# Four layers on one core: a matmul product in another bank, operators built later, a branch flag read earlier, and a fifth buffer

## The chip, the cores and the metric

The kernel runs on one core of one Trainium2 chip. The time is the device time in microseconds of one execution; a kernel's time is the median of several runs. A profile of one execution gives the spans and waits that are quoted. TensorE (PE) multiplies matrices, VectorE (DVE) and ScalarE (ACT) work on vectors, GpSimd (POOL) does slower vector work and issues some transfers, SyncE (SP) issues most transfers.

## The reference

The input is eight images of 512 channels by 32 by 32 pixels, in float32. Four layers follow each other:

- Layer 0: group norm over 8 groups; q, k, v by 512 x 512 weights; attention with 8 heads over the 1024 pixels; then three times `hf = hf + 0.1 * tanh(hf @ inl_w.T + inl_b)`; a 512 x 512 projection; and the layer's input is added.
- Layer 1: attention with one head, with 64 channels for q and k and 512 for v; and its input is added.
- Layer 2: a bias; upsampling by two with a 12-tap filter in both directions; leaky ReLU times the square root of two; downsampling by two with a 12-tap filter.
- Layer 3: the mean of each channel gives, through a router and a sigmoid, the weights of eight experts; the mixed kernels are used in a 1x1, a 3x3 and a 1x1 convolution, each with its scale and bias, ReLU after the first two; the layer's input is added, and a last ReLU follows.

## The kernel before, in words

`tile_sequence` computes all of it. A first loop goes over the images: `layer0`, `layer1`, and `layer2` for all but the last image; the results of layer 2 are spilled to DRAM. Then comes `layer2` of the last image, and a loop over the images for layer 3. The code gives a program order; the planner of the tile framework decides how the instructions of different stages are mixed on each engine, and each engine then takes its own in that order. A tile is taken from a ring of buffers; it can be written when the readers of the ring's buffer are done.

The rings that matter here. PSUM has three: `ps_mm` and `ps_tp` with two banks each, `ps_sc` with two pairs of banks. In SBUF, `big` has seven buffers, `tmp` of 1024 columns has four, `half` (a `tmp` of 512 columns) two.

The large products are done with seven half-size products in place of eight (`product`): from the four quarters of the weights and of the data it forms sums (`weight_sums` on GpSimd, `quarter_sums` on DVE), and adds up the seven products P1, C11, U2, U3, C22, C21, C12 in three pairs of banks, A (from `ps_mm`), X and Y (from `ps_sc`). P1 and C11 need no sums of the data. The trace names these banks: `inl_A`, `inl_X` and `inl_Y` are those of the inner loop, whatever the iteration.

In layer 0's attention a group is two heads and half of the query pixels. `weighted` adds its product in one bank of `ps_mm`; `normalised` takes one bank of `ps_tp` for the totals (L638), the reciprocal (L642), and multiplies into `hf` (L643), which reads and so frees the `ps_mm` bank. The inner loop's first product follows the last group. Its A banks are both from `ps_mm`.

Layer 2 is done by matmuls with small operators: `up_left_op`, `up_op`, `up63_op` for upsampling, `dn_op`, `dn63_op` for downsampling. `layer2_constants` builds them from the filters' taps, with some 360 small DVE instructions on a scratch tile `setup`, and clears the border rows of the padded image in DRAM (`ypad`, by `rim0`). It is called in layer 1 of the first image, ahead of the scores. `weighted_rows` is layer 1's product of weights and values (its matmuls are the `av` of L853, its sums are `av_U`, `av_W`, `av_P`); layer 2's matmuls are `up` (L919) and `dn` (L940), and `leak` (L902 on ACT, L903 on DVE) reads the upsampling banks.

No maximum is subtracted ahead of the exponentials. In place of it, GpSimd adds all their sums into `seen`; at the end, the kernel counts whether all are within a bound, loads the answer into a register of each engine (L1175), and a branch (L49) repeats everything with shifts where they are not. With the inputs used it isn't taken.

Of the kernel before, what the change touches and what calls it, by code (L numbers as in the profile page):

```python
# [9 lines left out]
F32 = mybir.dt.float32  # L10
BF16 = mybir.dt.bfloat16
AF = mybir.ActivationFunctionType
ALU = mybir.AluOpType
AX = mybir.AxisListType
# [3 lines left out]
P = 128  # L18
B, C, H, W = 8, 512, 32, 32
S = H * W  # L20
CC = C // P
SC = S // P
HALF = 512
# [18 lines left out]
BOUND = 1e20  # L42
# [11 lines left out]
def tile_sequence(ctx: ExitStack, tc: tile.TileContext, a: dict, out: bass.AP, shifted: bool):  # L54
    nc = tc.nc
# [4 lines left out]
    work = ctx.enter_context(tc.tile_pool(name=f"work_{run}", bufs=2))  # L60
    small = ctx.enter_context(tc.tile_pool(name=f"small_{run}", bufs=4))
    spill = ctx.enter_context(tc.tile_pool(name=f"spill_{run}", bufs=1, space=DRAM))
    ps_sc = ctx.enter_context(tc.tile_pool(name=f"ps_sc_{run}", bufs=2, space=PSUM))
    ps_tp = ctx.enter_context(tc.tile_pool(name=f"ps_tp_{run}", bufs=2, space=PSUM))
    ps_mm = ctx.enter_context(tc.tile_pool(name=f"ps_mm_{run}", bufs=2, space=PSUM))

    def big_tile(name, shape):
        return big.tile(shape, F32, tag="big", name=name)

    def bank(pool=None, name="mm"):  # L70
        pool = pool or ps_mm
        return pool.tile([P, HALF], F32, tag="bank", name=name)

    def tmp(name, n=HALF):
        if n == HALF:
            return work.tile([P, n], F32, tag="half", name=name, bufs=2)
        return work.tile([P, n], F32, tag="tmp", name=name, bufs=4)

    def sums(name):
        return work.tile([P, S], F32, tag="sums", name=name, bufs=2)  # L80
# [50 lines left out]

    def layer2_constants():

        setup = big_tile("setup", [P, CC * S])
        used = [0]

        def scratch(name, n):
            used[0] += n
            return setup[:, used[0] - n : used[0]]

        def iota(name, pattern, base, per_partition=0):
            t = scratch(name, pattern[0][1])
            nc.gpsimd.iota(
                t, pattern, base=base, channel_multiplier=per_partition,
                allow_small_or_imprecise_dtypes=True,
            )
            return t

        def placed(name, idx, taps):
            n = idx.shape[1]  # L150
            t, one = scratch(f"placed_{name}", n), scratch(f"one_{name}", n)
            for k in range(NTAP):
                dst = t if k == 0 else one
                nc.vector.tensor_scalar(
                    dst, idx, float(k), taps[:, k : k + 1], ALU.is_equal, ALU.mult
                )
                if k:
                    nc.vector.tensor_add(t, t, one)
            return t

        taps_up = scratch("taps_up", NTAP)
        nc.gpsimd.dma_start(taps_up, a["up_filter"].partition_broadcast(P))
        nc.vector.tensor_scalar_mul(taps_up, taps_up, 2.0)
        taps_dn = scratch("taps_dn", NTAP)
        nc.gpsimd.dma_start(taps_dn, a["down_filter"].partition_broadcast(P))

        part = iota("part", [[1, 1]], 0, 1)

        def rows_of(name, width):

            row, step = scratch(f"row_{name}", 1), scratch(f"step_{name}", 1)
            nc.vector.memset(row, 0.0)
            for k in range(width, P, width):
                nc.vector.tensor_scalar(step, part, float(k), None, ALU.is_ge)
                nc.vector.tensor_add(row, row, step)
            col = scratch(f"col_{name}", 1)
            nc.vector.scalar_tensor_tensor(col, row, float(-width), part, ALU.mult, ALU.add)
            return row, col

        def tap_index(name, n, step, base, mul, by):  # L180

            t = iota(f"ix_{name}", [[step, n]], base)
            add = scratch(f"add_{name}", 1)
            nc.vector.tensor_scalar_mul(add, by, float(mul))
            nc.vector.tensor_scalar_add(t, t, add)
            return t

        def outer(op, rows, cols):
            nr, ncol = rows.shape[1], cols.shape[1]
            nc.vector.tensor_tensor(  # L190
                op.rearrange("p (r c) -> p r c", c=ncol),
                rows.unsqueeze(2).to_broadcast([P, nr, ncol]),
                cols.unsqueeze(1).to_broadcast([P, nr, ncol]),
                ALU.mult,
            )

        in_c, in_r = rows_of("in", IR)
        ur = placed("ur", tap_index("ur", UR, -1, 17, -2, in_r), taps_up)
        outer(up_op, ur, placed("uc", tap_index("uc", UC, 1, 11, -2, in_c), taps_up))
        outer(
            up_left_op, ur, placed("ucl", tap_index("ucl", UC, 1, 11 - 2 * EDGE, -2, in_c), taps_up)
        )
        up_rr, up_cc = rows_of("up", UC)  # L210
        outer(
            dn_op,
            placed("dr", tap_index("dr", OR, 2, -6, 1, up_rr), taps_dn),
            placed("dc", tap_index("dc", OC, 2, 0, -1, up_cc), taps_dn),
        )
        in_c, in_r = rows_of("in63", 3)
        outer(
            up63_op,
            placed("ur63", tap_index("ur63", 1, 0, 10, -2, in_r), taps_up),
            placed("uc63", tap_index("uc63", 2 * W, 1, 5, -2, in_c), taps_up),  # L220
        )
        outer(
            dn63_op,
            placed("dr63", iota("dr63", [[2, 3]], 1), taps_dn),
            placed("dc63", tap_index("dc63", W, 2, 6, -1, part), taps_dn),
        )

        rim0 = tmp("rim0")
        nc.vector.memset(rim0, 0.0)
        for t in ypad:  # L230
            nc.gpsimd.dma_start(t[0 : 3 * W], rim0[0 : 3 * W])
            nc.gpsimd.dma_start(t[(H + 3) * W :], rim0[0 : 2 * W])


    ypad = [
        spill.tile([(H + 5) * W, C], F32, name=f"ypad_{run}_{i}", tag=f"ypad_{i}") for i in range(2)
    ]


    pooled = const.tile([P, CC, B], F32, name="pooled")  # L240
# [138 lines left out]
            nc.vector.tensor_sub(t[3][cc], t[1][cc], b21)  # L379
        return t  # L380

    def product(name, wt, src, sums_of, made, rows=False):

        banks = {
            "A": [bank(name=f"{name}_A{u}") for u in range(2)],
        }
        for key in "XY":
            two = ps_sc.tile([P, S], F32, tag="scores", name=f"{name}_{key}")  # L390
            banks[key] = [two[:, ts(u, HALF)] for u in range(2)]
# [30 lines left out]
    def all_of(gen):  # L422
        for _ in gen:
            pass
# [141 lines left out]
    def layer0(b, x, norm, w):  # L566
# [11 lines left out]
        w["proj"] = weight("proj", b)  # L578
        all_of(product(f"v_{b}", w["v"], h, t, positions(f"v_{b}", v, v_row), rows=True))
        w["v1"] = weight("v1", b)  # L580

        hf = big_tile(f"hf_{b}", [P, CC, S])
        rows = [slice(HD * r, HD * r + HD) for r in range(2)]
        shifts = None
# [73 lines left out]
        for it in range(3):  # L658
            t = quarter_sums(f"hf_{b}_{it}", hf, None if it else v)
            name = f"inl_{b}_{it}"  # L660
            all_of(product(name, w["inl"], hf, t, inner_step(name, hf)))
        if b + 1 < B:
            w["q"] = weight("q", b + 1)
        t = quarter_sums(f"hf_{b}_3", hf)
# [4 lines left out]
    def layer1(b, x, w, midway):  # L669
# [29 lines left out]
            )  # L699
        v = big_tile(f"v1_{b}", [P, SC, C])  # L700
        eT = [big_tile(f"eT_{b}_{sh}", [P, SC, HALF]) for sh in range(2)]
        if b == 0:
            layer2_constants()
        inv = small.tile([P, SC], F32, tag="inv1", bufs=2, name=f"inv1_{b}")
        accs = {}

# [74 lines left out]
                midway()  # L781

        weighted_rows(b, eT, v, inv, y, written)
        for t in range(3, NT):
            halo.load(t)
        halo.load_last()
# [299 lines left out]
    def mixed(b):  # L1086
# [10 lines left out]
                )  # L1097
        return wt

    z3 = {}  # L1100

    def freed(t):
# [8 lines left out]

    z_last = layer2(B - 1, halo, freed)
    z_next = z3[0]
    wt_next = mixed(0)
    route(B - 1, B)
    for b in range(B):
# [28 lines left out]
        for oc in range(CC):  # L1145
            at = C + 9 * P + oc * P
            ps = ps_sc.tile([P, S], F32, tag="scores", name=f"c3_{b}_{oc}")
            for g in range(2):
                nc.tensor.matmul(
                    ps[:, ts(g, HALF)], wt[:, at : at + P], h2[:, ts(g, HALF)],  # L1150
                    start=True, stop=True,
                )
            n = S if b + 1 < B else HALF
            for part in range(S // n):
                dst = z[:, oc, ts(part, n)]
                nc.vector.scalar_tensor_tensor(
                    dst, ps[:, ts(part, n)], bn[2][0][:, oc : oc + 1], dst, ALU.mult, ALU.add
                )
                nc.scalar.activation(dst, dst, AF.Relu, bias=bn[2][1][:, oc : oc + 1])
            nc.sync.dma_start(out[b, ts(oc, P), :], z[:, oc, :])  # L1160

    if shifted:
        return None

    within = tmp("within")
    nc.vector.tensor_scalar(within, seen, BOUND, None, ALU.is_le)
    count = small.tile([P, 1], F32, tag="count", name="count")
    nc.vector.tensor_reduce(count, within, AX.X, ALU.add)  # L1170
    ps = bank(name="within")
    nc.tensor.matmul(ps[0:1, 0:1], count, ones[:, 0:1], start=True, stop=True)
    redo = small.tile([P, 1], mybir.dt.int32, tag="redo", name="redo")
    nc.vector.tensor_scalar(redo[0:1, :], ps[0:1, 0:1], P * HALF - 0.5, None, ALU.is_lt)
    return nc.values_load(redo[0:1, 0:1], min_val=0, max_val=1)  # L1175


def _layout(inp):
# [64 lines left out]
```

## Time and profile before

| what | us |
|---|---|
| time, median of three runs | 3965.67 |
| lowest and highest | 3965.24, 3966.4 |
| span of the profiled execution | 3956.6 |
| DVE busy | 2592.0 |
| ACT busy | 1104.7 |
| GpSimd busy | 437.9 |

The span goes from the first to the last instruction of the profiled execution. A line of the timeline gives the start, the duration, the engine, the line of the kernel, the operation, what it writes from what it reads, the shape and how many were joined; in brackets, how long the engine had been idle and what ended that. The view of waits sums such idle times by pairs. The chain of work goes back from the last instruction to what released each step. A float32 matmul appears as two passes, each counted.

### The profile page before, as it was taken

The numbers are of one execution on the slowest core, as the hardware profiler recorded it, in microseconds if no ns is written. First come the engines' busy times: TensorE is split into PE (matmuls) and PEld (weight loads), VectorE is DVE, ScalarE is ACT, GpSimd is POOL, SyncE is SP. The second block draws the span as 40 slices with busy tenths as digits, with TensorE's granted clock in tenths as the row PEclk, the third lists the DMA queues.
The fourth block names the chain that finished last, engine by engine and source line by source line (L and its number), as shares of the span: only waits on it lengthen the run. The fifth ranks groups of instructions, "written<-read, shape, count | busy, mean of one in ns | idle before, by whom it ended". The sixth has DMA issues, their size and how long they took to land.

```text
span 3956.6 us, 37918 instructions
## 1 busy us (share of the span) xinstructions
PE 3873.8 (98%) x14630; PEld 2036.0 (51%) x14630; DVE 2592.0 (66%) x3690; ACT 1104.7 (28%) x1507; POOL 437.9 (11%) x310
## 2 busy tenths in 40 slices
PE   8998999999999999999999999999999999999998
PEld 4335753476435763367434764357534764346543
DVE  4779548764676647765486646765477655766885
ACT  1421214212332114212241223322142123321332
POOL 5310003000120003100030002200030001201000
PEclk9999999999999999999999999999999999999999
DMA  5002310113101310023101220013200131003432
GB/s 189 19 7 78 105 71 1 40 62 114 38 1 59 117 59 19 0 83 114 56 1 58 75 85 36 0 69 107 78 1 24 61 115 54 1 0 115 159 140 95
DMA packets 85214, 247.85 MB, mean 63 GB/s; under 512 B 10416, under 2 KB 32960, under 8 KB 78240
## 3 DMA queue, kind: packets, MB, share of 16 engines
q1 hardware_dynamic: 69136, 220.23, 15.6%
q10 hardware_dynamic: 13824, 12.59, 0.9%
q0 software_dynamic: 2064, 12.51, 0.8%
q8 instruction: 117, 1.92, 0.2%
q14 instruction: 73, 0.60, 0.0%
HBM read 185.40 MB, written 59.90 MB: 62 GB/s over the span
## 4 chain that ended last, share of the span: by engine, by line
PE 91%; DVE 6%; ACT 1%; DMA 1%; issue 1%; POOL 0%; ACTq 0%; SPq 0%; DVEq 0%; POOLq 0%
PE scores L264 13%; PE av L628 11%; PE inl_X L414 6%; PE dn L940 6%; PE up L919 5%; PE v_X L414 4%; PE inl_Y L414 4%; PE av_X L853 4%; PE inl_A L414 3%; PE c L1135 3%; PE v_Y L414 3%; PE av_Y L853 3%; PE av_A L853 2%; PE proj_X L414 2%; PE q_X L414 2%; PE k_X L414 2%
## 5 line engine op out<-in xcount | busy, mean ns | idle before, releaser
L613 ACT ACTIVATE e<-scores 128x1024 f32<-128x1024 f32 x512 | 497.4, 1022 | 583.0 <-PE scores L264 580.3
L619 DVE TENSOR_TENSOR acc<-acc,e 128x1024 f32<-128x1024 f32 x384 | 494.0, 1287 | 123.5 <-ACT e L613 103.4
L264 PE MATMUL scores<-q,k 64*128 64x512 f32 x2048 | 511.1, 616 | 6.0 <-DVE v L495 3.3
L628 PE MATMUL av<-e,v 128*64 128x512 f32 x2048 | 494.2, 605 | 0.0
L645 POOL TENSOR_TENSOR seen<-seen,acc 128x512 f32<-128x512 f32 x128 | 213.6, 1669 | 1565.0 <-DVE acc L619 1560.0
L264 PEld LDWEIGHTS scores<-q,k 64*128 64x128 f32 x2048 | 176.0, 186 | 333.1 <-ACT e L613 162.1
L628 PEld LDWEIGHTS av<-e,v 128*64 128x64 f32 x2048 | 124.9, 136 | 338.7 <-issue 336.4
L903 DVE SCALAR_TENSOR_TENSOR up<-up,leak 128x512 f32<-128x512 f32 (+1 forms) x264 | 174.5, 686 | 141.8 <-ACT leak L902 136.5
L940 PEld LDWEIGHTS dn<-dn_op,up 128*128 128x128 f32 (+1 forms) x2048 | 240.2, 192 | 44.0 <-issue 24.2
L940 PE MATMUL dn<-dn_op,up 128*128 128x126 f32 (+5 forms) x2048 | 244.7, 275 | 7.6 <-DVE up L903 6.8
L642 DVE RECIPROCAL inv<-total 128x512 f32<-128x512 f32 x64 | 214.7, 3355 | 0.0
L902 ACT ACTIVATE leak<-up 128x512 f32<-128x512 f32 (+1 forms) x264 | 150.1, 595 | 208.2 <-DVE up L903 131.0
L414 PE MATMUL inl_A<-hf,w_inl 128*128 128x512 f32 x384 | 178.0, 599 | 10.7 <-DVE hf L643 10.7
L919 PE MATMUL up<-halo,up_op 126*128 126x512 f32 (+1 forms) x384 | 182.6, 604 | 0.9 <-DVE up L903 0.8
L414 PE MATMUL inl_X<-T_hf,w_inl 128*128 128x512 f32 x384 | 175.2, 592 | 0.0
L645 POOL TENSOR_TENSOR seen<-seen,inv 128x512 f32<-128x512 f32 x64 | 125.2, 1956 | 416.9 <-DVE inv L642 416.9
L617 DVE TENSOR_TENSOR acc<-e,e 128x1024 f32<-128x1024 f32 x64 | 83.0, 1297 | 102.5 <-ACT e L613 102.5
L508 ACT ACTIVATE inl_U<-inl_U,inl_b 128x512 f32<-128x512 f32 x96 | 66.7, 718 | 287.4 <-DVE inl_U L523 287.4
L519 DVE TENSOR_TENSOR inl_U<-inl_X,inl_P 128x512 f32<-128x512 f32 x96 | 61.8, 685 | 111.4 <-PE inl_X L414 111.4
L737 POOL TENSOR_TENSOR seen<-seen,acc 128x512 f32<-128x512 f32 x16 | 23.4, 1461 | 987.7 <-DVE acc L729 921.5
L414 PEld LDWEIGHTS inl_A<-hf,w_inl 128*128 128x128 f32 x384 | 70.4, 190 | 110.2 <-issue 95.3
L1135 PE MATMUL c<-rim,mixed 128*128 128x512 f32 x288 | 124.9, 592 | 0.0
(302 smaller groups left out, 5779.0 us busy)
## 6 DMA issues: line engine op xcount, KB each, us to landing
halo<-ypad_u SPq DMA_DIRECT2D x128, 252.0 KB
halo<-ypad_u SPq DMA_DIRECT2D x128, 198.0 KB
w_v<-stored_u_v SPq DMA_DIRECT2D x14, 1792.0 KB
x<-in_x_dram SPq DMA_DIRECT2D x32, 512.0 KB
out_dram<-z SPq DMA_DIRECT2D x32, 512.0 KB
spill_u<-z SPq DMA_DIRECT2D x28, 512.0 KB
z<-spill_u SPq DMA_DIRECT2D x28, 512.0 KB
w_q<-stored_u_q SPq DMA_DIRECT2D x7, 1792.0 KB
```

Source lines behind the costliest of these rows:

```text
L264: nc.tensor.matmul(ps[r], k[r], q[r], start=True, stop=(shift is None))
L414: nc.tensor.matmul(dst, lhs, rhs, start=(opens and s == 0 and cc == 0), stop=(cc == 1 and s == rows), skip_group_check=True,)
L613: nc.scalar.activation(e, ps, AF.Exp, scale=HD ** -0.5)
L619: nc.vector.tensor_add(accs[g], accs[g], e)
L628: nc.tensor.matmul(avs[g][rows[r]], v[:, jc, ts(2 * oc + r, HD)], e[:, ts(r, HALF)], start=(jc == 0), stop=(jc == SC - 1),)
L642: nc.vector.reciprocal(inv, ps)
L645: nc.gpsimd.tensor_add(seen, seen, part)
L853: nc.tensor.matmul(ps[:, ts(s, QR)], left[:, j, at : at + P], right[:, j, :], start=(what in ("P1", "U2", "W") and s == 0 and j == 0), sto ...
L903: nc.vector.scalar_tensor_tensor(dst, ps, SQRT2, t, ALU.mult, ALU.max)
L919: nc.tensor.matmul(ps[i], op[0 : IR * n, :], halo.tile(t)[0 : IR * n, c + i, :], start=True, stop=True,)
L940: nc.tensor.matmul(rows[:, r0 - first : r1 + 1 - first, c0 : c1 + 1], up[t][0:k, c, ts(cc, P)], op[:, r0 - 4 * t + 3 : r1 + 4 - 4 * t, c0 ...
L1135: nc.tensor.matmul(banks[g].rearrange("p (h w) -> p h w", w=W), wt[:, at : at + P], h1[:, ky + 16 * g : ky + 16 * g + 16, kx : kx + W], st ...
```

## The change

Four edits, and some that go with them:

- The inner loop's first product takes its A banks one from `ps_mm` and one from `ps_tp`, the ring of the totals, so that neither is the one that the last group's `av` still holds.
- `layer2_constants` is called after `weighted_rows`, shortly ahead of the layer that needs the operators. Its scratch tile is a `tmp` of 1024 columns in place of a `big` one. Clearing the border rows is taken out of it and put at the beginning of the kernel.
- The flag for the branch is worked out after layer 2 of the last image, ahead of layer 3's loop, in a function `out_of_bounds`; the last image's output is written in halves of a channel block, as each is ready. In the built program, SyncE's load of the flag stands ahead of the load of the second image for layer 3; on the other engines the load is still the last instruction ahead of the branch.
- `tmp` has five buffers.

```
-        return work.tile([P, n], F32, tag="tmp", name=name, bufs=4)
+        return work.tile([P, n], F32, tag="tmp", name=name, bufs=5)
...
     def layer2_constants():
-        setup = big_tile("setup", [P, CC * S])
+        setup = tmp("setup", S)
...
-        rim0 = tmp("rim0")
-        nc.vector.memset(rim0, 0.0)
-        for t in ypad:
-            nc.gpsimd.dma_start(t[0 : 3 * W], rim0[0 : 3 * W])
-            nc.gpsimd.dma_start(t[(H + 3) * W :], rim0[0 : 2 * W])
...
+    rim0 = tmp("rim0")
+    nc.vector.memset(rim0, 0.0)
+    for t in ypad:
+        nc.gpsimd.dma_start(t[0 : 3 * W], rim0[0 : 3 * W])
+        nc.gpsimd.dma_start(t[(H + 3) * W :], rim0[0 : 2 * W])
...
-        banks = {
-            "A": [bank(name=f"{name}_A{u}") for u in range(2)],
-        }
+        banks = {"A": first_banks or [bank(name=f"{name}_A{u}") for u in range(2)]}
...
-            all_of(product(name, w["inl"], hf, t, inner_step(name, hf)))
+            banks = None if it else [bank(p, f"{name}_A{u}") for u, p in enumerate((ps_mm, ps_tp))]
+            all_of(product(name, w["inl"], hf, t, inner_step(name, hf), first_banks=banks))
...
-        if b == 0:
-            layer2_constants()
...
         weighted_rows(b, eT, v, inv, y, written)
+        if b == 0:
+            layer2_constants()
...
     z_last = layer2(B - 1, halo, freed)
     z_next = z3[0]
+    redo = None if shifted else out_of_bounds()
     wt_next = mixed(0)
...
-            nc.sync.dma_start(out[b, ts(oc, P), :], z[:, oc, :])
-    if shifted:
-        return None
-    within = tmp("within")
...
-    return nc.values_load(redo[0:1, 0:1], min_val=0, max_val=1)
+                nc.sync.dma_start(out[b, ts(oc, P), ts(part, n)], dst)
+    return redo
```

The part of the old end that is cut above (comparison, count, one matmul, and the load into registers) is the body of `out_of_bounds`, with its bank from `ps_tp`.

More of the change, by code (lines that the diff above doesn't have):

```diff
@@ L138, in scratch @@
             used[0] += n
+            assert used[0] <= S, used
             return setup[:, used[0] - n : used[0]]
@@ L380, in quarter_sums, with product @@
         return t
-    def product(name, wt, src, sums_of, made, rows=False):
-        banks = {
-            "A": [bank(name=f"{name}_A{u}") for u in range(2)],
-        }
+    def product(name, wt, src, sums_of, made, rows=False, first_banks=None):
+        banks = {"A": first_banks or [bank(name=f"{name}_A{u}") for u in range(2)]}
         for key in "XY":
@@ L1098, in mixed, with out_of_bounds @@
         return wt
+    def out_of_bounds():
+        within = tmp("within")
+        nc.vector.tensor_scalar(within, seen, BOUND, None, ALU.is_le)
+        count = small.tile([P, 1], F32, tag="count", name="count")
+        nc.vector.tensor_reduce(count, within, AX.X, ALU.add)
+        ps = bank(ps_tp, "within")
+        nc.tensor.matmul(ps[0:1, 0:1], count, ones[:, 0:1], start=True, stop=True)
+        redo = small.tile([P, 1], mybir.dt.int32, tag="redo", name="redo")
+        nc.vector.tensor_scalar(redo[0:1, :], ps[0:1, 0:1], P * HALF - 0.5, None, ALU.is_lt)
+        return nc.values_load(redo[0:1, 0:1], min_val=0, max_val=1)
     z3 = {}
@@ L1159, in tile_sequence @@
                 nc.scalar.activation(dst, dst, AF.Relu, bias=bn[2][1][:, oc : oc + 1])
-            nc.sync.dma_start(out[b, ts(oc, P), :], z[:, oc, :])
-    if shifted:
-        return None
-    within = tmp("within")
[L1168 to L1175, printed above, removed]
+                nc.sync.dma_start(out[b, ts(oc, P), ts(part, n)], dst)
+    return redo
 def _layout(inp):
```

## The prediction

> **What bounds the kernel now.** I read the page's busy times first, then the chain that ended last, then who TensorE waited for, and then the timeline of each place that the change touches.
>
> ```profile
> PE 3873.8 (98%) x14630; PEld 2036.0 (51%) x14630; DVE 2592.0 (66%) x3690; ACT 1104.7 (28%) x1507; POOL 437.9 (11%) x310
> PE 91%; DVE 6%; ACT 1%; DMA 1%; issue 1%; POOL 0%; ACTq 0%; SPq 0%; DVEq 0%; POOLq 0%
> ```
>
> TensorE is busy in 3873.8 of 3956.6 us and is 91% of the chain. No matmul is removed, so all there is to win is its 82.8 us of idleness, the slow clock after a long stop, and the tail. Who ends that idleness:
>
> ```profile
> PE inl_A L414 <- DVE hf L643: 10.7, 7, 1.5
> PE v_X L414 <- DVE setup L174: 9.0, 1, 9.0
> PE total L638 <- DVE acc L619: 8.6, 8, 1.1
> PE av_X L853 <- DVE av_U L827: 3.1, 1, 3.1
> PE v_X L414 <- DVE v_U L488: 2.6, 1, 2.6
> ```
>
> The columns are total us, times, longest. The first row is the inner loop's bank wait, in seven of eight images. The rows of one time each belong to image 0's layer 1, where layer 2's operators are built. The total of what that costs is read from the chain, between the same two points of image 0 and image 1 (start, us, what):
>
> ```profile
> 297.00 6.01 PE proj_A L414 x14
> 449.34 10.34 PE dn L940 x92
> ...
> 775.73 6.01 PE proj_A L414 x14
> 905.94 10.34 PE dn L940 x92
> ```
>
> 449.34 - 297.00 = 152.3 us against 905.94 - 775.73 = 130.2: image 0 loses 22.1 us, more than its waits, because matmuls after a stop are slow:
>
> ```profile
> 346.93 0.27 DVE L190 TENSOR_TENSOR up_left_op<-setup 128x128 f32<-128x128 f32 x1
> 347.26 1.13 PE L264 MATMUL scores<-qk 64*128 64x512 f32 x4
> ...
> 350.14 0.27 DVE L190 TENSOR_TENSOR dn_op<-setup 128x126 f32<-128x126 f32 x1
> ...
> 357.34 5.82 PE L414 MATMUL v_X<-w_v,T_x 128*128 128x256 f32 x16 [8.96 <-DVE setup L174]
> ```
>
> The same sixteen matmuls take 3.72 us elsewhere. DVE began the operators at 330.61, so their part up to up_left_op is 16.5 us and up to dn_op 19.7 us of uninterrupted DVE.
>
> **What the Trainium skill says.** "TensorE: Matmul & The Clock Gate", section "What's actually happening": after an idle window of about 3.4 us the array runs at half clock until it has been busy for about as long. The 5.82 instead of 3.72 us above agrees, and so does 5.41 us after the 3.06 us stop for av_U. Its section "Architectural detail" says that ScalarE and VectorE are strictly first in, first out: what is queued behind a waiting DVE instruction waits as well. "SBUF — State Buffer", "SBUF: two separate sides": DVE with two SBUF inputs and GpSimd lock each other out; at the start a 512-wide subtraction takes 1.75 us while GpSimd sums weights and 0.68 us after it.
>
> **Part 1, the inner loop's first product.** Before, the second bank of A is the one that av of the last group holds until L643 has read it. In the third image:
>
> ```profile
> 1157.17 1.99 PE L414 MATMUL inl_A<-hf,w_inl 128*128 128x512 f32 x4
> 1159.98 3.34 DVE L642 RECIPROCAL inv<-total 128x512 f32<-128x512 f32 x1
> 1164.08 1.20 DVE L377 TENSOR_TENSOR v<-hf,v 128x512 f32<-128x512 f32 x1
> 1164.19 1.96 PE L414 MATMUL inl_A<-hf,w_inl 128*128 128x512 f32 x4 [1.52 <-DVE hf L643]
> ```
>
> A product of 512 columns is two passes, 0.86 us. Before, six products (A, A, X, A, A, Y) fill 1157.17 to 1162.67, then 1.52 us pass. After, the two banks are av's free one and that of the previous total, and the built program's order is eight A products and then X. Two A end at 1158.99, eight at 1158.99 + 6 x 0.86 = 1164.15, the ninth product (X of the first chunk, whose operand was subtracted early) at 1165.0; the tenth needs L377, whose end stays at 1165.28, so it starts at about 1165.35 with nine done. Before, at that time 6 + (1165.35 - 1164.19) / 0.86 = 7.35 are done. Gain 1.65 x 0.86 = 1.42 us. In image 0 the border's memset (0.41 us between two starts) also leaves DVE's chain, and the 0.77 us wait for L377 with it: nine products end at 230.31 where eight are done at 230.64, 1.2 us. Sum 7 x 1.42 + 1.2 = 11.1 us. What follows is not bound by DVE: L519 may read X while two Y products (1.7 us) run. The wait of total for acc (8.6 us) stays; its order is unchanged.
>
> **Part 2, the operators.** The stretch from layer 1's scores to the sums in weighted_rows loses its operators and should run as in image 1. They now stand on DVE behind the batch statistics of image 1, among the last av sums. I put the costs of the before trace (0.066 to 0.07 us for a 128x1 step, 0.08 to 0.14 for wider ones; they give 16.6 and 19.8 us, as measured) on the new order, in image 1's times. DVE is free at 873.1. 173 operator instructions (16.7 us) and 7.7 us of av sums stand ahead of up_left_op's end, so it is there at 873.1 + 24.4 = 897.5. TensorE, whose upsampling products no longer stand among the av ones, ends av at 883.55 + 24 x 0.43 = 893.9: a wait of 3.6 us. Its next four products go to 901.2; then comes gn_var, which needs gdev, and gdev stands on DVE behind 90 more operator instructions (8.5 us) and 2.1 us of other work: 907.7, a wait of 6.5 us. The same queue holds the leaks (L903) that free the upsampling banks: the first at 908.1, the fourth done at 912.6, the sixth at 914.0, each 0.6 us. So upsampling ends at about 916.3, where image 1 has its block of 92 dn matmuls begin at 905.3 (four of them having gone ahead): 11 us late, plus about 1 us of slow clock after the two stops (about 1.7 to 2.2 us are lost by each such stop in the trace, but most of it lies within the later waits). The last 56 operator instructions (6.5 us) lie beside the dn block (10.3 us). Gain 22.1 - 12 = 10 us. Bounds: 5 if bank and leak waits pile up, 14 if DVE gets through in the gaps.
>
> **Part 3, the flag.** Comparison and sum are 0.42 and 0.68 us on DVE, now beside layer 2's last downsampling; the mixed weights that they delay are needed 7 us later than they are ready (w3 done at 3723.5, used at 3731.6). The matmul (two passes of 0.16 us) is moved, not added. SyncE's read of the flag comes ahead of the load of z of image 1: that waits a microsecond or two from 3706.8 on and is needed at 3737.8.
>
> ```profile
> 3941.16 5.54 SPq L1160 DMA_DIRECT2D out_dram<-z  x4
> ```
>
> ```profile
> L1175 SPq TENSOR_LOAD <-redo x1: 507/507/507, 3946.8 to 3946.8; - x1
> ```
>
> At the end, SyncE's load, register operations and check (to 3947.6, 0.9 us) go. The last image's four writes of 512 KB, one each 1.72 us, become eight of 256 KB at 0.86 us, so the last one has 256 KB, about 0.85 us at that rate, less to move. These overlap partly, and ACT's own load (1.13 us) still ends near 3947: 1.0 us, between 0 and 2.
>
> **Part 4, the rest.** The fifth buffer removes no wait of TensorE that the list shows, so I price it at nothing. The border's memset moves into the start, between gmul and gadd (0.2 to 0.43 us), and its four writes (0.55 us each) hold GpSimd's weight sums by up to 1.3 us, which lengthens their overlap with the T_h subtractions: +0.7 us, between 0.3 and 1.7.
>
> Sum: -11.1 - 10 - 1.0 + 0.7 = -21.4; 3965.67 - 21.4 = 3944.3 us.
>
> **The rivals.** (a) The operators' stop merely moves: up_left_op, gn_var and the leaks together cost as much as before. For it: 35 us of DVE work still stand in one queue, and TensorE takes gn_var in order. Against: image 1's DVE is busy only 10.7 of 20 us there. With a gain of 2 instead of 10: 3952.3. (b) Part 1's wait is moved to X, since the reciprocal (3.34 us) and three DVE steps end when they did. For it: U2 needs L377. Against: eight A products last 6.9 us. If 0.3 us an image remain, 2.4 in all: 3953.0. (a) and (b) together: 3961.0. (c) Slower: SyncE stands at the flag while the loads of z queue behind it. If the flag came only with layer 3's first image, near 3737, the 8 us load would come some 9 us late and the gains would be lost elsewhere: 3974.7. Against it: its last input, GpSimd's sums, ends with layer 1. (d) Better: bounds of 14 for part 2, 2 for the tail, 0.3 for the start: 3938.9.
>
> **How the numbers follow.** Forecast 0.57, (d) 0.15, (a) 0.11, (b) 0.10, both 0.05, (c) 0.02. The all-good sum (part 1 at 12.5) is 28.2, 3937.5; the all-bad (8 + 5 - 1.7) is 11.3, 3954.4: range 3937 to 3954. Faster by over 0.2% means below 3957.7: 0.93; same 0.05; slower 0.02.
>
> **What would show it.** Right: the row of inl_A waiting for L643 is gone, and eight inl_A products stand together; the stops for setup, v_U and av_U are gone, and in their place are stops of 3 to 7 us for up_left_op, gdev and L903 at image 0's upsampling; from proj_A to dn image 0 takes about 142 us. Wrong: a new row of inl_X waiting for L377 at 1 us or more an image, over 147 us in image 0, or TensorE idle in layer 3.

## The result and the profile after

The changed kernel takes 3937.74 us (median of six runs, 3936.17 to 3950.39) against 3966.03 us for the kernel before (3965.24 to 3970.29): a ratio of 0.9932, 95% interval 0.9919 to 0.9946. The forecast was 3944.3 us, its range 3937 to 3954. The two profiled executions have spans of 3956.6 and 3934.4 us, 22.2 us apart.

The page's busy line and the chain's shares by engine, of the kernel after:

```profile
PE 3868.2 (98%) x14630; PEld 2032.6 (52%) x14630; DVE 2593.8 (66%) x3690; ACT 1105.0 (28%) x1507; POOL 436.1 (11%) x310
PE 90%; DVE 7%; issue 1%; DMA 1%; ACT 1%; SPq 0%; DVEq 0%; ACTq 0%
```

TensorE still bounds the kernel. Its idle time went from 82.8 to 66.2 us and its busy time from 3873.8 to 3868.2 us. Of the rows that say who ends that idle time now, these bear on the change (total, times, longest, in us):

```profile
PE dn L941 <- DVE up L904: 9.5, 7, 5.6
PE total L637 <- DVE acc L618: 8.6, 8, 1.1
PE gn_var L296 <- DVE gdev L294: 7.3, 2, 6.5
PE inl_X L414 <- DVE v L379: 1.4, 8, 0.2
PE av_X L854 <- DVE av_W L833: 0.9, 1, 0.9
```

The rows of inl_A waiting for hf, of v_X for setup and v_U, and of av_X for av_U are gone; the total's wait for acc is unchanged. New are one stop of 6.5 us at gn_var and, ahead of it, three stops of 0.8 to 0.9 us among the last av products of image 0 (one row is shown). The timeline of image 2 shows the first edit: the sixteen passes (eight products) of inl_A in one run, and 0.18 us of waiting at X where 1.52 us stood at A.

```profile
1146.93 7.13 PE L414 MATMUL inl_A<-hf,w_inl 128*128 128x512 f32 x16
1153.90 1.02 PE L414 MATMUL inl_X<-v,w_inl 128*128 128x512 f32 x2
1155.10 2.84 PE L414 MATMUL inl_X<-v,w_inl 128*128 128x512 f32 x6 [0.18 <-DVE v L379]
```

The timeline of image 0, where layer 2 begins, shows what the operators cost in their new place:

```profile
429.69 0.59 PE L296 MATMUL gn_var<-gdev,group_mean 128*128 128x4 f32 x2 [6.46 <-DVE gdev L294]
430.14 2.05 PE L920 MATMUL up<-halo,up_left_op 99*128 99x512 f32 x2
...
435.33 1.12 PE L920 MATMUL up<-halo,up_left_op 99*128 99x512 f32 x2
...
438.87 10.86 PE L941 MATMUL dn<-dn_op,up 112*128 112x66 f32 x96
```

gn_var stands behind the operators on VectorE's queue, and the two passes after the stop take 2.05 us where the same two take 1.12 us five microseconds later. The block of dn begins late, but as one block of 96, since nothing of it could go ahead.

To see where the time went, both executions are divided at the first matmul of q_A, inl_A and av_A of each image, at the first c (layer 3's first product) and at the last c. Each number is a difference of start times in the timeline; the first row begins with the span, and the last ends with it.

| stage, us | before | after |
|---|---|---|
| up to the first q_A | 14.96 | 15.13 |
| image 0: q_A to inl_A | 207.51 | 209.24 |
| image 0: inl_A to the next q_A | 276.38 | 264.53 |
| images 1 to 7: q_A to inl_A, sum | 1412.02 | 1413.05 |
| images 1 to 7: inl_A to av_A, sum | 982.44 | 969.09 |
| images 1 to 7: av_A to the next q_A (or c), sum | 813.81 | 816.46 |
| first to last c | 236.42 | 236.42 |
| last c to the end | 13.05 | 10.46 |

The row of 813.81 and 816.46 holds no edit but the fifth buffer, and it differs between executions (below). Without it the gain is 24.9 us.

### The profile page after: what moved, and what is told of

It is laid out like the page before. It is cut to its first block, busy times and chain, and to the rows that moved or that the text cites. A ratio compares the mean times of both kernels' runs of the same rounds, so it can differ in the third digit from the quotient of the medians.

```text
span 3934.4 us, 37957 instructions
## 1 busy us (share of the span) xinstructions
PE 3868.2 (98%) x14630; PEld 2032.6 (52%) x14630; DVE 2593.8 (66%) x3690; ACT 1105.0 (28%) x1507; POOL 436.1 (11%) x310
## 4 chain that ended last, share of the span: by engine, by line
PE 90%; DVE 7%; issue 1%; DMA 1%; ACT 1%; SPq 0%; DVEq 0%; ACTq 0%
PE scores L266 13%; PE av L627 11%; PE inl_X L414 6%; PE dn L941 6%; PE up L920 5%; PE v_X L414 4%; PE inl_Y L414 4%; PE av_X L854 4%; PE c L1150 3%; PE v_Y L414 3%; PE av_A L854 3%; PE v_A L414 3%; PE inl_A L414 3%; PE av_Y L854 2%; PE proj_X L414 2%; PE q_X L414 2%
## 5 line engine op out<-in xcount | busy, mean ns | idle before, releaser
L414 PE MATMUL inl_A<-hf,w_inl 128*128 128x512 f32 x384 | 169.5, 594 | 0.0
```

The source lines that it names most:

```text
L414: nc.tensor.matmul(dst, lhs, rhs, start=(opens and s == 0 and cc == 0), stop=(cc == 1 and s == rows), skip_group_check=True,)
```

## The experiments

The theory after the result (A): the parts add up, 11 to 12 us for the bank, 8 to 10 for the operators and what goes with them (a start about 2 us longer counted in), 2 to 3 for the tail. Its rivals: the fifth buffer or the mixture brings a good part (B), and those named in each text. Times of the kernel before, beside these runs, were 3967.0 us in the first group (e1 to e4), 3965.1 in the second (e5 to e8), 3967.75 and 3966.93 for the rest.

**e1, the bank alone.** Of the change only this:

```
-            all_of(product(name, w["inl"], hf, t, inner_step(name, hf)))
+            banks = None if it else [bank(p, f"{name}_A{u}") for u, p in enumerate((ps_mm, ps_tp))]
+            all_of(product(name, w["inl"], hf, t, inner_step(name, hf), first_banks=banks))
```

> The kernel before with the first product's banks alone changed. Theory A (the gain of the whole change is the sum of its parts, and what it has over the forecast is the granted clock, which differs from run to run): 11 to 12 us less than before, 1.5 in each of seven images and 1.2 in the first, so about 3954.5 beside 3966; no row of inl_A waiting for L643, and a row of inl_X waiting for the sums at under 0.3 us an image. Theory B (the fifth buffer or the mix of parts brings the rest): the same here. Rival (the wait moves to X): 2 to 3 us less, 3963.

Measured: 3949.85 us, ratio 0.9958 (0.9945 to 0.9972), 17 us by the medians. inl_A to av_A falls from 140.35 to 138.44 us in each of images 1 to 7, as in the whole change, and by 1.66 us in image 0 (1.90 between e2 and the whole change): 15.0 us in all, where 11 to 12 were expected. The wait did not move to X, as the rival had it: inl_X waits 0.2 us an image. Besides the stop at L643, another went. The timelines of v_A, the product for layer 1's values, in image 2, of the kernel before and then of e1:

```profile
1262.31 5.34 PE L414 MATMUL v_A<-w_v,x 128*128 128x256 f32 x24
1267.90 2.00 PE L414 MATMUL v_A<-w_v,x 128*128 128x256 f32 x8 [0.24 <-ACT v_P L478]
```

```profile
1256.71 7.17 PE L412 MATMUL v_A<-w_v,x 128*128 128x256 f32 x32
```

Likely the bank taken from the other ring shifts which bank each later product gets, so that v_A no longer meets one that ScalarE is still copying from; the stop is shown to go with this edit, the reason for it wasn't tried.

**e2, the operators alone**, with what goes with them (scratch on a temporary buffer, the zeros at the start, five buffers):

```
-        setup = big_tile("setup", [P, CC * S])
+        setup = tmp("setup", S)
...
         weighted_rows(b, eT, v, inv, y, written)
+        if b == 0:
+            layer2_constants()
```

> The kernel before with the operators late on a tmp scratch, the border cleared at the start, and the fifth buffer that the scratch takes. Theory A: 10.6 us less for the operators and 1.9 more at the start, net 8 to 10 less, about 3957. Theory B: 14 to 16 us less, 3951, since the buffer brings some 6 of it. In the profile image 0's upsampling shows a stop of about 6.5 us at gn_var.

Measured: 3959.62 us, ratio 0.998 (0.9972 to 0.9988), 7.4 us. inl_A to the next q_A of image 0: 267.24 against 276.38 us, and the start 3.6 us longer in this execution. The stop at gn_var is there, 6.5 us. The median's gain is just under A's 8 to 10 us and far from B's 14 to 16.

**e3, the flag and the halves of the output; e11, the flag alone; e8, the halves alone.** The edit of e8 and of e3:

```
-            nc.sync.dma_start(out[b, ts(oc, P), :], z[:, oc, :])
+                nc.sync.dma_start(out[b, ts(oc, P), ts(part, n)], dst)
```

and of e11 and e3:

```
+    redo = None if shifted else out_of_bounds()
...
-    return nc.values_load(redo[0:1, 0:1], min_val=0, max_val=1)
+    return redo
```

> The kernel before with the flag worked out ahead of layer 3 and the last image's output in halves. Theory A: 2.5 us less, all after the last 3x1 block of layer 3, so about 3963.5 beside 3966. Theory B: the same. Rival (the flag is hidden at the end and costs SyncE in layer 3): 0, 3966.

> Only the write of the output in halves is taken from the change; the branch flag is still loaded at the end, and nothing is left out. Theory A (the tail of e3, 9.98 us from the start of the last c matmul to the end against 13.05 before, is shortened by both): halves bring about 0.7 us, since the last transfer starts one half of z earlier and is half as large, and the load of the flag the remaining 2.3 us: the tail takes 12.0 to 12.7 us. Rival (the transfers set the end, the load lies beside them): the tail takes 10.0 to 10.5 us.

> Only the early load of the branch flag is taken from the change; the output is written whole, and nothing is left out. The tail from the start of the last c matmul to the end took 13.05 us before, 11.41 with the halves alone, 9.98 with both. Theory A (the two add up): 11.5 to 12 us. Rival (the load stands after the last transfer's issue and only the halves shorten the end, the rest being a spread of the last landings): 12.7 to 13.1 us.

Measured: e3 3962.05 us (0.9988, 0.998 to 0.9997), e8 3963.14 (0.9995, 0.9987 to 1.0003), e11 3963.35 (0.9989, 0.9981 to 0.9997). By these medians alone e8 can't be told from no change; the profiles show more. From the last c to the end: 9.98 us with both, 11.41 with the halves, 9.06 with the flag, and 12.96 to 13.07 in the four profiles with neither (before, e1, e2, e4). Neither theory for e8 nor for e11 held: the flag alone shortens the end by 4.0 us, more than with the halves added. The instructions that close the program on GpSimd's queue (POOLq) and SyncE's (SPq) show where the time goes. A line gives the count, the shortest, median and longest in ns, and the first and last start; before, and then e11:

```profile
L1239 POOLq DRAIN  x3: 40/107/3013, 3952.8 to 3956.3; - x3
L1239 SPq DRAIN  x3: 7/7/13, 3953.4 to 3956.0; - x3
```

```profile
L1239 POOLq DRAIN  x3: 40/107/3013, 3724.8 to 3962.6; - x3
L1239 SPq DRAIN  x3: 7/7/13, 3962.0 to 3962.3; - x3
```

GpSimd closes with an instruction of 3.01 us. Before, it begins 3.8 us ahead of the end, after the branch that waited for the flag, and ends last: SyncE's first closing instruction is through 3.2 us ahead of the end. With the flag read early, GpSimd has nothing left to do from layer 3 on and runs it 238 us ahead of the end, and SyncE closes 0.9 us ahead of the end. So, by these starts, GpSimd accounts for 3.2 - 0.9 = 2.3 us of the 4.0, and SyncE's own earlier closing for the other 1.7 (9.9 us after the last c begins, against 8.2). In the changed kernel GpSimd's instruction starts at 3694.8 as well.

**e4, the fifth buffer alone; e10, the change without it.**

```
-        return work.tile([P, n], F32, tag="tmp", name=name, bufs=4)
+        return work.tile([P, n], F32, tag="tmp", name=name, bufs=5)
```

> The kernel before with five buffers for tmp and nothing else. Theory A: within 1 us of before once the granted clock is the same, 3966. Theory B: 5 to 7 us less, 3960.

> The changed kernel with four temporary buffers instead of five, the scratch of the operators still one of them; nothing is left out. Theory A (the fifth only stands in for the one that the scratch holds): the same in images 1 to 7 (stages within 0.7 us), and in image 0 up to 6 us more where leak waits for a buffer, 3937 to 3945 us. Rival (the fifth is worth something in every image): 0.3 us or more in each image's stages, 3941 to 3950 us. Rival C (the fifth does nothing): 3936 to 3939 us.

Measured: e4 3964.64 us (0.9993, 0.9985 to 1.0002), e10 3937.94 us, beside 3937.74 for the change. B falls: the buffer brings nothing. The median of e10 is where rival C had it, though also within A's 3937 to 3945. The buffer even costs a little: q_A to inl_A is 201.77 against 201.72 us in e4, and the sum over images 1 to 7 is 1413.05 us in the change and 1412.05 in e10.

**e7, the zeros later.** The changed kernel with these lines just before the inner loop of image 0 instead of at the start:

```
+        if b == 0:
+            rim0 = tmp("rim0")
+            nc.vector.memset(rim0, 0.0)
...
         for it in range(3):
             t = quarter_sums(f"hf_{b}_{it}", hf, None if it else v)
```

> The changed kernel with the zeros of the padded rows (one memset and four transfers) emitted just before the inner loop of image 0 instead of at the start; nothing is left out. Theory A (these are what made the start 1.9 us slower: first q_A of image 0 to inl_A 209.24 us, 207.51 before): q_A to inl_A of image 0 returns to 207.5 us, the rest as in the changed kernel, so 1.5 to 2 us below it, 3935 to 3936 us by the median. Rival (the start differs between executions by the granted clock): q_A to inl_A of image 0 stays at 208.5 us or more.

Measured: 3934.19 us, ratio 0.9926 (0.9912 to 0.9939), slightly below A's 3935 to 3936. q_A to inl_A of image 0 is 207.53 us, as A had it.

**e5, the operators before the inner loop; e6, late with their own scratch.** Both give the scratch a constant buffer and go back to four temporary buffers. e5 moves the call, and the clearing of the border rows with it; e6 leaves both where the change has them. The scratch, and the call of e5:

```
+    setup = const.tile([P, S], F32, name="setup")
...
-        setup = tmp("setup", S)
...
+        if b == 0:
+            layer2_constants()
         for it in range(3):
```

> The changed kernel, with the operators of layer 2 (and the zeros of the padded rows) emitted between the attention and the inner loop of image 0, on a constant buffer of their own, and four temporary buffers; nothing is left out. Theory A (the operators cost time only where VectorE has no room beside TensorE; in the changed kernel that is the end of layer 1 of image 0, where inl_A to dn takes 214.5 us in image 0 and 197.2 in image 2): VectorE has room in the products and the attention of image 0, the stop of TensorE for gdev (6.5 us) and the slow matmuls after it go, so inl_A to dn of image 0 takes 197 to 203 us, the start loses its +1.9 us, and the median is 3921 to 3928 us. Rival B (wherever they stand, the 430 small operations delay VectorE by about as much as TensorE then waits): the lag shows up as scores, total or inl_X waiting on VectorE in image 0, and the median is 3935 to 3942 us.

> The changed kernel with four temporary buffers, the scratch of the operators on a constant buffer of its own; nothing is left out. Theory A (the fifth buffer only replaces the one that the scratch holds until its last use): the same as the changed kernel within its spread, 3936 to 3943 us, and every stage within 0.7 us of the changed kernel's. Rival (the fifth buffer helps in every image): at least 2 us more over images 2 to 7.

Measured: e5 3940.52 us, e6 3937.65 us. Half of A held in e5: inl_A to the next q_A of image 0 is 252.67 us, the lag is gone. But q_A to inl_A is 223.75 us, 16.2 more than the 207.53 of e7, so the median is where B had it. The timeline of e5, image 0:

```profile
62.19 6.28 PE L412 MATMUL k_X<-T_h,w_k 128*128 128x512 f32 x8 [6.82 <-DVE k_U L442]
...
84.94 3.44 PE L412 MATMUL v_A<-w_v,h 128*128 128x256 f32 x8 [2.47 <-DVE setup L174]
```

The operators ran beside the products for k and v, long before the place of the call. They also took longer there: the 362 instructions that build them keep VectorE busy for 50.2 us in e5, the 361 of the changed kernel for 40.0. Ten of them take 0.8 to 1.3 us in place of 0.15 to 0.25, each while GpSimd forms weight sums, and each is through within 0.06 us of the end of one such sum. One of them and its sum:

```profile
82.37 1.25 DVE L185 TENSOR_SCALAR setup<-setup 128x32 f32<-128x32 f32 x1
```

```profile
82.32 1.26 POOL L358 TENSOR_TENSOR w_proj<-w_proj 128x512 f32<-128x512 f32 x1
```

So the 16.2 us need not be the price of the operators alone; how much of it goes to GpSimd's sums was not tried. e6 did not test what it was meant to: its call is late, but its operators ran early too (q_A to inl_A 225.64 us), so that its median is where A had it for another reason. e10 and e6 differ only in the scratch's buffer: with a temporary one the operators run from 395 us on, at the end of layer 1; with one of their own nearly all run between 40 and 120 us. So it is the temporary buffer, for which they must wait, that holds them late in the changed kernel.

**e9, the operators in four pieces.** e7, with a temporary buffer for each piece, so that each is held where it is called:

```
         def piece(name):
+            place.update(tile=tmp(f"setup_{name}", HALF), used=0)
...
             all_of(product(name, w["inl"], hf, t, inner_step(name, hf), first_banks=banks))
+            next(pieces, None)
...
         t = quarter_sums(f"hf_{b}_3", hf)
+        next(pieces, None)
```

> The changed kernel with the zeros of the padded rows just before the inner loop of image 0 (as in e7), and the operators of layer 2 in four pieces, each with a temporary buffer of its own, emitted after the three steps of the inner loop and at the start of the projection of image 0; nothing is left out. Theory A (40 us of small operations cost nothing where VectorE has room beside TensorE, and cost time when they come in one block, as at the start in e5 and at the end of layer 1 in the changed kernel): inl_A to dn of image 0 falls from 214.5 us to 197 to 203 us, the stops for gdev and av_U, av_W, av_P go, q_A to inl_A stays at 207.5 us, but dn to q_A rises from 50.0 to about 55.4 us as in the other images (work of layer 2 that the stop had let in early), so the gain over e7 is 6 to 12 us: a median of 3922 to 3928 us. Rival B (the operators cost TensorE the same wherever they stand): the stops come back as inl_X or proj waiting on VectorE, and the median is 3931 us or more.

Measured: 3931.39 us, ratio 0.9912 (0.9898 to 0.9925), 6.3 us below the changed kernel by the medians and 2.8 below e7; B had it at 3931 us or more, A at 3922 to 3928. inl_A to dn is 203.68 us, and image 0 from its first q_A to the next takes 467.19 us, against 473.10 in e7 and 473.77 in the changed kernel. That is a smaller gain than A's, and some of B's stops are there. From the waits of e9, and the sum line of its windows over 210 to 350 us:

```profile
PE inl_X L419 <- DVE setup_up L180: 1.8, 1, 1.8
PE proj_X L419 <- DVE setup L179: 1.0, 1, 1.0
```

```profile
sum 140.00, PE 135.13 PEld 61.34 DVE 131.82 ACT 32.13 POOL 9.73; mean PE 19.30 PEld 8.76 DVE 18.83 ACT 4.59 POOL 1.39
```

VectorE is busy in 131.82 of these 140 us: the operators, 362 instructions that keep it busy for 46.0 us here, nearly fill what room there was. From inl_A to dn image 0 still takes 6.5 us longer than image 2 (197.2 us).

**e12, e9 with the output written whole.**

```
-                nc.sync.dma_start(out[b, ts(oc, P), ts(part, n)], dst)
+            nc.sync.dma_start(out[b, ts(oc, P), :], z[:, oc, :])
```

> The kernel of e9 with the output written whole instead of in halves; nothing is left out. The tail from the start of the last c matmul to the end took 13.05 us before, 9.06 with the early flag alone (e11), 11.41 with the halves alone (e8), 9.74 to 10.73 with both (five kernels). Theory A (with the flag early the end waits only for the last transfers, and twice as many of them land later): 8.9 to 9.3 us, and a median 0.5 to 1.5 us below e9, about 3930.5 us, whose spread from run to run is larger. Rival B (e11 was one short tail of a spread; halves do no harm): 9.7 to 10.5 us, the median as in e9.

Measured: 3930.88 us (3928.68 to 3931.26), ratio 0.9906 (0.989 to 0.9923), the lowest median of all. The end takes 9.10 us, as A had it (8.9 to 9.3). With the flag early, two profiles without halves show 9.06 and 9.10 us, and seven with halves 9.74 to 10.73: there the halves cost 0.6 to 1.7 us. That e12 is faster than e9 is seen in the end's profile; the medians are too close to show it.

## Why the prediction was right, and where it was off

**Part 1, forecast 11.1 us, measured 15.0.** The step itself came out to the hundredth. Nine products should be done 8.18 us after inl_A's start (1165.35 - 1157.17); the third line of image 2 above begins at 1155.10 - 1146.93 = 8.17 us with nine done. Mis-sized was the gain, which the forecast ended at that point with "What follows is not bound by DVE": it counted no stop for ScalarE and priced every product at 0.86 us. v_A's stop for the copy by ScalarE also went, 0.24 us an image. And four groups of inl_A, alternating with X and Y, took 1.82, 1.80, 1.79 and 1.80 us from start to start before, where sixteen passes in one run take 6.97: another 0.24 us. With 1.52 - 0.18 = 1.34 us for the stop this is 1.82 of the measured 1.91 us an image; the forecast had 1.42. Rival (b), by its sum, left only 0.3 us an image of the gain and moved the rest to X; with a wait of 0.18 us there it did not come.

**Part 2, forecast 10 us, measured 10.2.** The change and e1 give 276.38 - 264.53 - 1.66. These are single profiles, and this stretch differs between executions: it takes 276.38 to 279.36 us in the five with bank and operators as before (before, e3, e4, e8, e11) and 264.53 to 265.57 in the three with both edits (the change, e7, e10). So 10.2 stands for something between 9 and 13, and that it meets the forecast so closely is in part luck. The three steps of the working can be checked in the timeline, set back to image 1's times by av_A's start (478.03 us later): up_left_op is done at 897.5 us (forecast 897.5), gn_var begins at 907.7 (907.7), the dn block at 916.9 (916.3). One reading of the forecast was off: image 1's block of dn begins not at 905.3 but here:

```profile
905.77 10.50 PE L940 MATMUL dn<-dn_op,up 112*128 112x84 f32 x92
```

By it the forecast has the block 10.5 us late, and the measured one is 11.1 us late. Only the first stop was much smaller, 0.4 instead of 3.6 us: TensorE had been held up on the way at three of the last av products, by 0.8 to 0.9 us each (for av_U, av_W, av_P), which the forecast did not have. Together with the 0.4 us these are 3.0 us, so TensorE goes on at the same time. That the lag of image 0 is only moved, rival (a), is refuted by e2 and the table.

**Part 3, forecast 1.0 us, measured 2.6** (2.3 to 3.3 over the seven profiles with both edits). The term that was wrong is what the early flag removes: the forecast took SyncE's 0.9 us of loading and checking, and left out GpSimd, which stands behind the same branch with 3.0 us of closing work, 2.3 of them on the path. The halves were counted as a gain; alone they are one (13.05 to 11.41 us), beside the early flag they are a loss.

**Part 4, forecast +0.7 us, measured +1.9, and +1.0 for the fifth buffer.** The cause of the first was right, as e7 shows, and the size is just past the bad end of 0.3 to 1.7. It is all in q_A's wait for h, 2.38 us where it was 2.00, and in the waits for T_h; before, and then after:

```profile
26.87 2.84 PE L414 MATMUL q_X<-T_h,w_q 128*128 128x512 f32 x6 [1.27 <-DVE T_h L377]
```

```profile
26.03 1.10 PE L414 MATMUL q_X<-T_h,w_q 128*128 128x512 f32 x2 [1.11 <-DVE T_h L379]
28.81 2.84 PE L414 MATMUL q_X<-T_h,w_q 128*128 128x512 f32 x6 [1.69 <-DVE T_h L379]
```

The subtractions that make T_h take 1.75 us beside GpSimd's weight sums and 0.68 after them, as the forecast has it: two take 1.75 us before, four after. The buffer was put at nothing, since it removes no wait; it costs 0.05 us an image, and with the operators at the end of layer 1 another 0.66 us in image 1. Why it costs anything was not tried.

The sum is -15.0 - 10.2 - 2.6 + 1.9 + 1.0 = -24.9 us against -21.4. That the time comes out near rival (d), 3938.9 us, is no sign for it: of its terms only the tail's reached its bound, and the start went the other way. The medians are 28.3 us apart, with an interval of about 21 to 32. The measured 3937.74 us is only 0.7 us inside the forecast's range of 3937 to 3954, less than the spread of its six runs: that it lies inside is luck in part, though the mechanisms of parts 1, 2 and of the start are as forecast.

**What remains** of that difference is likely in a stage that hardly any edit touches. The sum from av_A to the next q_A of images 1 to 7 lies between 813.46 and 826.42 us in the fourteen profiled executions, and the profile of the kernel before happens to have one of the lowest (813.81) and a shorter time, 3958.48 us, than all 34 of its later runs in the first group (3960.4 to 3974.89). So 22.2 us between the two profiles is too little, and the timed medians are the better measure. The timed runs have no stages, so the remaining 3.4 us are not placed.

## What to carry to other kernels

Work that only has to be done once is not free because its engine is "66% busy": the same operators cost TensorE 16 us beside the first products, where some of them also took longer beside GpSimd's sums, 12 us at the end of layer 1 and some 6 us in pieces over an inner loop. So divide such work and look at the room in each stage. The place of a call in the source alone does not hold work late: with a scratch of its own it ran more than 300 us earlier, with a buffer of a shared ring it stayed. When a wait is taken from the end of a program, look at every engine that stands behind the same branch, not only the one that loads the flag.

## What the runs showed of the hardware that was not expected

TensorE's slow clock also follows stops that are each shorter than those in the prediction. The Trainium skill, "TensorE: Matmul & The Clock Gate", section "What's actually happening", puts it after an idle window of about 3.4 us. Here trace and page differ. In e1, image 5, two stops of 1.18 and 0.89 us with 0.46 us of work between them were enough; the granted clock is 1.00 from 2725 to 2730 us, 0.56 in the next 5 us and 0.75 in the 5 after those (timeline of e1, then the same block in the kernel before):

```profile
2729.32 0.46 PE L939 MATMUL dn<-dn_op,up 128*128 128x99 f32 x2 [1.18 <-DVE up L902]
2730.68 11.95 PE L939 MATMUL dn<-dn_op,up 128*128 128x126 f32 x76 [0.89 <-DVE up L902]
```

```profile
2734.23 8.73 PE L940 MATMUL dn<-dn_op,up 128*128 128x126 f32 x76 [0.44 <-DVE up L903]
```

The same 76 passes take 3.2 us longer. Such a stop does not come in every image, nor in the same images of each execution, and of the stages that the edits leave alone this one differs most between the profiled executions. The changed kernel's six runs go from 3936.17 us at a mean clock of 0.998 to 3950.39 us at 0.995. What makes VectorE late there was not tried.
